# First attention step turned by TensorE, second step's keys gathered in layer 1, and two inverse roots taken as powers on GpSimd

## The chip, the cores and the metric

The kernel runs on one core of a Trainium2 chip. The core has five engines that run side by side and wait for one another only through semaphores: TensorE (PE, matrix products and transposes, which write to the PSUM memory), VectorE (DVE), ScalarE (ACT, among other things exponentials), GpSimd (POOL) and SyncE (SP, which here only issues DMA transfers). The profile keeps TensorE's loading of the stationary operand apart as PEld. The metric is the device time of one execution in microseconds (us), lower is better. The kernel before was timed three times.

## The reference, cut to what matters

The program is a chain of four layers over x, 8 sequences of 128 tokens with 512 features, all in float32. Layers 0 and 1 are feed-forward layers with low-rank experts, layer 2 is attention over a paged cache of keys and values followed by a small expert layer, layer 3 is again feed-forward. The change touches the end of layer 1 and the start of the attention:

```python
q = rmsnorm(x @ Wq.T) * q_norm_w          # 32 heads of 128
k = rmsnorm(x @ Wk.T) * k_norm_w          # 8 key heads of 128
v = x @ Wv.T
q, k = rope(q, pos), rope(k, pos)         # rotary: t * cos +- (other half of t) * sin
kc, vc = k_cache[block_table], v_cache[block_table]      # 512 cached positions
scores = q @ concat(kc, k).T / sqrt(128)
probs = softmax(where(valid, scores, -1e30))
x = x + layer(probs @ concat(vc, v) @ Wo.T)
# rmsnorm(t) = t * rsqrt(mean(t * t) + 1e-6)
```

## The kernel before

*Steps.* The attention runs in 32 steps, n = 0 to 31, each one key head (with its four query heads, REP) and a pair of sequences. A step needs, in this order: its projection (`project`, by a seven-product scheme written in `seven`, whose products are named q_one, q_six, q_five), the inverse root-mean-squares of its heads (`squares`, `roots`, `normed`), the rotation (`rotate`, `rotated`), the queries and new keys turned so that the head's 128 features lie along the partitions (`turn`, `fetch`), the cached keys gathered from the cache (`gather`, "kn") and turned likewise (`turn_cached`, "kt", "kT"), the score products (`weigh`, tile st, L1132) with their exponentials, and the mixing with the values (`mix`, tile av, L1184). The output products wo_one, wo_two and wo_six of step n - 1 stand between those of step n + 1's projection and the second half of step n.

*Order.* Nearly all attention instructions are issued with `keep_in_program_order`, so each engine runs them in the order of the text. The functions passed in the dictionary `at` (keys "one", "u2", "c22", "c11", "c12") are called by `seven` after the product of that name, and so say where on every engine's queue other work is put. `issue_after` keeps instructions behind a named one. Pools with `bufs` give a tile a new buffer only when its last users are done; the bank tags "av" (two), "st" and "mm" (three each) hold PSUM, and the tags "kt", "qT", "r" have one buffer each, "kn" two.

*Turning through memory.* VectorE's transpose works on blocks of 32x32. `turn` therefore transposes the blocks of `both` (eight query heads and two key heads, 128x1280) on VectorE, writes the result to a DRAM tensor in four DMAs (`written`, L1102), and `fetch` reads it back rearranged (L1119 for qT, L1122 for the keys kn). The cached keys go the same way (L1093, L1102, L1098).

*The transition (L1242 to L1299).* Layer 1's last steps interleave with the attention's start. `begin` loads weights and gathers step 0's keys and values on GpSimd. `first` projects step 0, turns its cached keys, gathers step 1's keys, starts to project step 1, and at "one" of that projection runs `rest`: squares and roots of step 0 on ScalarE, layer 1's last outputs (eo_l, added into x by VectorE at L300), rotation and norm of step 0, and its turning, for which half of the writes are issued by ScalarE. `run` then issues three matmuls into idle_q whose result is not used, the squares of step 1 on ScalarE, step 1's rotation, its cached keys, its roots, norm and turning, and then goes round the steps.

*Roots.* `roots` is a Sqrt on ScalarE (L1079), which needs another function table than Exp, and `normed` has VectorE's reciprocal (L1085) before the product with the queries (L1086). The key's root is the scale of the exponential of the new keys.

Of the kernel before, what the change touches and what calls it, by code (L numbers as in the profile page):

```python
# [10 lines left out]
F32 = mybir.dt.float32  # L11
I32 = mybir.dt.int32
AF = mybir.ActivationFunctionType
# [34 lines left out]
def forward(ctx: ExitStack, tc: tile.TileContext, a: dict, out: bass.AP):  # L48
# [252 lines left out]

    def block_masked(dst, ps, mask, g):

        dve.tensor_tensor(
            dst.rearrange("p (b t) -> p b t", t=P),
            ps.rearrange("p (b t) -> p b t", t=P),
            mask[:, 4 * g : 4 * g + 4].unsqueeze(2).to_broadcast([P, 4, P]),
            ALU.mult,
        )
# [358 lines left out]
    with psa:  # L668
        c2 = psa.enter_context(ExitStack())
        ps_ = psa.enter_context(tc.tile_pool(name="psa", bufs=2, space=PSUM, reuse_waits="tile"))  # L670
        sums = nc.dram_tensor("sums", (HQ * NB // REP, REP * P), F32, kind="Internal").ap()

        def small_bank(shape, name):
            return ps_.tile(shape, F32, tag="av", name=name)

        def large_bank(shape, name):
            return ps_.tile(shape, F32, tag="st", name=name, bufs=3)


        att = attention(tc, a, x, ident, lens, kvrow, part, ww, wop, ypool, sums, rot, eps, ps_, c2, chunks, mm)  # L680

        l1 = att.scratch([P, DC * P + NT], "l1")
        wa1 = l1[:, 0 : DC * P].rearrange("p (c r) -> p c r", c=DC)
        sp.dma_start(wa1, chunks(a["wa1"]))
        t1 = l1[:, DC * P : DC * P + NT]

        def adapt(g):
            tok = slice(g * 512, (g + 1) * 512)
            ps = small_bank([P, 512], f"t1_{g}")
            for c in range(DC):  # L690
                mm(ps, wa1[:, c, :], x[:, c, tok], c == 0, c == DC - 1)
            block_masked(t1[:, tok], ps, mask1, g)

        mids1, route1, mix1, outs1 = experts(
            "l1", None, None, 16.0, br.unsqueeze(1).to_broadcast([P, NB, 8]), wB1, None, None, add_to_x,
            mid_of=lambda tok: [(t1[:, tok], w11)],
        )[:4]

        mix0(0, large_bank)
        outs0(0, (0, 1), large_bank)  # L700
        mids0(1, small_bank)
        route0(1)
        outs0(0, (2, 3), large_bank)
        mix0(1, small_bank)
        outs0(1, (0, 1), large_bank)
        adapt(0)
        outs0(1, (2, 3), large_bank)
        mids1(0, small_bank)
        route1(0)
        att.begin()  # L710
        adapt(1)
        mix1(0, small_bank)
        outs1(0, range(DC), large_bank)
        mids1(1, small_bank)
        route1(1)
        att.first(lambda: mix1(1, small_bank), lambda *o: outs1(1, o, large_bank))
        kept = nc.dram_tensor("kept_x", (P, DC, NT), F32, kind="Internal").ap()
        c1.close()
        cl = ExitStack()
        late = cl.enter_context(tc.tile_pool(name="late", bufs=1, side="right"))  # L720

        def bank(tag, shape, name):
            return ps_.tile(shape, F32, tag=tag, name=name, bufs=2 if tag == "av" else 3)

        def room(tag, shape, name):

            return (ypool if tag == "y" else wop).tile(shape, F32, tag=tag, name=name)

        def end_of(in_order):
            return ending(  # L730
                tc, a, out, x, ident, bias3, experts, late,
                lambda shape, name: ww.tile(shape, F32, tag="q7", name=name),
                lambda shape, name: ww.tile(shape, F32, tag="qs", name=name), room, chunks, mm, in_order,
            )

        y2, end = att.run(late, end_of, bank, lambda: sp.dma_start(kept, x))
        c2.close()
        c3 = ExitStack()
        w3 = c3.enter_context(tc.tile_pool(name="w3", bufs=1, reuse_waits="tile"))
        ex["sm"] = c3.enter_context(tc.tile_pool(name="sm3", bufs=2, side="right", reuse_waits="tile"))  # L740
        end.open3(w3, ex["sm"])
        end.layer2(y2, bank, do=range(NB - 2, NB))
# [49 lines left out]
def attention(tc, a, x, ident, lens, kvrow, part, ww, wop, ypool, sums, rot, eps, psa, c2, chunks, mm):  # L792
# [39 lines left out]
        tabs[m] = (ws, wx)  # L832


    vals = []
    for k in range(4):
        vals.append(ap.tile([P, NC, HD], F32, tag=f"vals{k}", name=f"vals{k}"))
# [198 lines left out]
    def squares(n, m, j, heads):  # L1036

        for i in heads:
            sq = wk.tile([P, HD], F32, tag="sq", name=f"sq{m}_{n}_{j}_{i}", bufs=1)
            col = i if m == "q" else REP  # L1040
            kept(act.activation(sq, S[n][m][:, j, i, :], AF.Square, accum_out=S[n]["ssq"][:, j, col : col + 1]))  # L1041

    def rotate(n):

        both = wk.tile([P, 2 * REP + 2, HD], F32, tag="r", name=f"r_{n}", bufs=1)
        views = {"q": both[:, 0 : 2 * REP], "k": both[:, 2 * REP :]}

        def terms(m, t, nh):

            full = [P, 2, nh, HD]  # L1050
            ws, wx = (w[:, pair(n), :] for w in tabs[m])
            r = views[m].rearrange("p (j h) d -> p j h d", j=2)
            u = wk.tile(full, F32, tag="v" + m, name=f"v{m}_{n}", bufs=1)
            for b in ((slice(0, 1), slice(1, 2)) if nh > 1 else (slice(0, 2),)):
                for lo, hi in ((0, 64), (64, 0)):
                    to = u[:, b, :, lo : lo + 64]
                    kept(pool.tensor_tensor(  # L1057
                        to, t[:, b, :, hi : hi + 64],
                        wx[:, b, lo : lo + 64].unsqueeze(2).to_broadcast(list(to.shape)), ALU.mult,
                    ))  # L1060
            def straight_terms():
                kept(dve.tensor_tensor(r, t, ws.unsqueeze(2).to_broadcast(full), ALU.mult))

            S[n]["r" + m] = r, u
            return straight_terms

        S[n]["both"] = both
        terms("q", S[n]["q"], REP)()
        return terms("k", S[n]["k"], 1)
# [6 lines left out]
    def roots(n):  # L1076
        s = S[n]
        s["rs"] = rs = wk.tile([P, 2, REP + 1], F32, tag="rs", name=f"rs_{n}")
        kept(act.activation(rs, s["ssq"], AF.Sqrt, bias=eps, scale=1.0 / HD))  # L1079

    def normed(n):

        s = S[n]
        r, rs = s["rq"][0], s["rs"]
        kept(dve.reciprocal(rs, rs))  # L1085
        kept(dve.tensor_tensor(r, r, rs[:, :, 0:REP].unsqueeze(3).to_broadcast([P, 2, REP, HD]), ALU.mult))  # L1086

    def turn_cached(n, tag="kt"):

        s = S[n]  # L1090
        t = wk.tile([P, 4, 8, 32], F32, tag=tag, name=f"kt_{n}", bufs=1)
        for j in range(2):
            kept(dve.transpose(  # L1093
                t[:, :, 4 * j : 4 * j + 4, :], s["kc"][j].rearrange("p c (b d) -> p b c d", b=4)
            ))
        s["kT"] = wk.tile([P, 4, 8, 32], F32, tag="kT", name=f"kT_{n}")
        written(turned[n], t)
        return lambda: kept(sp.dma_start(s["kT"], turned[n].rearrange("b i a m d -> (b i) a m d")))  # L1098
# [13 lines left out]
        written(turned_new[n], t, by)  # L1112
        return done

    def fetch(n, between=lambda: None):
        s = S[n]
        m = 2 * REP
        src = turned_new[n].rearrange("b i a m d -> (b i) a m d")
        kept(sp.dma_start(s["qT"], src[:, :, 0:m, :]))  # L1119
        between()  # L1120
        for j in range(2):
            kept(sp.dma_start(s["kn"][:, j], src[:, :, m + j, :]))  # L1122

# [118 lines left out]
    def begin():  # L1242
# [3 lines left out]
        gather(0, "v")  # L1246
        every(W[0].factors())

    def first(mixed, outs_):

        every(tokens(0))
        running.append(True)
        later = tokens(1, "pT")
        project(0, {
            "u2": lambda: turn_cached(0)(),
            "c22": lambda: every(later),
            "c11": lambda: (squares(0, "k", 0, (0,)), squares(0, "q", 0, (0, 1))),
            "c12": lambda: squares(0, "q", 0, (2, 3)),
        })
        keys_terms = rotate(0)  # L1260
        gather(1, "k")
        mixed()

        def rest():
# [2 lines left out]
            roots(0)  # L1267
            keys_terms()
            outs_(0)
            rotated(0)  # L1270
            outs_(1)
            normed(0)
            turned_0 = turn(0, (sp, act))
            fetch(0)
            with tc.issue_after(turned_0.ins):
                outs_(2, 3)

        project(1, {"one": rest})

    def run(pool_, end_of, bank, keep):  # L1280
        late.append(pool_)
# [1 line left out]
        Y.append(y2)  # L1283
        pool.memset(y2, 0.0)

        idle = psa.tile([P, 512], F32, tag="mm", name="idle_q", bufs=3)
        for _ in range(3):
            kept(pe.matmul(idle, x[:, 0, 0:P], x[:, 0, 0:512], start=True, stop=True))
        for j in range(2):
            squares(1, "q", j, range(REP))  # L1290
            squares(1, "k", j, (0,))
        keys_terms = rotate(1)
        read_cached = turn_cached(1, "xs")
        keys_terms()
        gather(1, "v")
        roots(1)
        rotated(1)
        normed(1)
        turn(1)  # L1299
# [6 lines left out]
        for n, (qd, p) in enumerate(steps):  # L1306
# [40 lines left out]
            summed(n, 0)  # L1347
            if n == 0:
                next(sums_of)
                fetch(1, read_cached)  # L1350
                gather(2, "k")
            every(sums_of)
            summed(n, 1)
# [36 lines left out]
        leave(n)  # L1390
        return y2, end

    return SimpleNamespace(begin=begin, first=first, run=run, scratch=scratch)


def rotary(tc, rp, tp, lens, part, rows, kept):
# [898 lines left out]
```

## Time and profile before

| what | value |
|---|---|
| three runs | 1494.15, 1496.87, 1497.94 us; median 1496.87 |
| profiled execution | 1495.56 us, of which the span from first to last instruction is 1493.8 us |
| granted clock of TensorE | 0.999 of full speed |
| TensorE busy | 1479.5 us, 99% of the span |
| VectorE, GpSimd, ScalarE busy | 1069.0, 848.5 and 565.6 us |
| score products of step 0 and of step 1 begin | 324.01 and 341.25 us after the span's start |

TensorE is busy nearly always, so a microsecond elsewhere counts only where TensorE ends up waiting for it. A timeline line gives start, duration, engine, line, operation, output<-inputs, the shape and how many instructions were merged; in brackets stands how long the engine was idle before and what ended that idle time. The durations of TensorE's instructions are modelled ends: in a stream, the distance from one start to the next is what counts.

### The profile page before, as it was taken

What the parts mean: (1) busy time and instruction counts of PE and PEld (TensorE: products, weight loads), DVE (VectorE), ACT (ScalarE), POOL (GpSimd) and SP (SyncE); (2) the same over time, 40 slices, a digit from 0 to 9 for tenths busy, and PEclk for the clock granted to TensorE, in tenths of its full rate; (3) what the DMA queues carried; (4) which work ended last, traced back from release to release, by engine and by line L of the source; (5) the groups of instructions that cost most, each with busy time, mean ns of one, the idle gap of its engine ahead of it and who ended that gap; (6) DMA issues with size and microseconds to landing.
All of it is one profiled execution on the core that took longest, in us unless ns stands there. A gap on an engine that the chain in (4) does not pass through costs nothing.

```text
span 1493.8 us, 18138 instructions
## 1 busy us (share of the span) xinstructions
PE 1479.5 (99%) x5615; PEld 940.4 (63%) x5615; DVE 1069.0 (72%) x2121; ACT 565.6 (38%) x1432; POOL 848.5 (57%) x869
## 2 busy tenths in 40 slices
PE   9999999999999999999999999999999999999998
PEld 7888787445555655555555555565555565559887
DVE  4665425388888787787778778787868878854475
ACT  1111101054545554454554444554444455431110
POOL 2241104377776777776777777677777677621210
PEclk9999999999999999999999999999999999999999
DMA  7311001145546444564454455345445534432001
GB/s 242 117 43 32 1 1 56 50 119 143 176 139 189 148 116 128 154 184 125 134 152 131 129 155 179 109 135 163 129 131 159 166 107 138 120 113 87 2 5 55
DMA packets 159305, 174.05 MB, mean 117 GB/s; under 512 B 54752, under 2 KB 129696, under 8 KB 159072
## 3 DMA queue, kind: packets, MB, share of 16 engines
q1 hardware_dynamic: 140768, 135.47, 30.8%
q0 software_dynamic: 17056, 36.49, 7.6%
q10 hardware_dynamic: 1376, 0.85, 0.2%
q8 instruction: 47, 0.77, 0.2%
q14 instruction: 58, 0.48, 0.1%
HBM read 130.66 MB, written 42.07 MB: 116 GB/s over the span
## 4 chain that ended last, share of the span: by engine, by line
PE 94%; DVE 3%; issue 1%; DMA 1%; ACT 0%; POOL 0%; SPq 0%; DVEq 0%; ACTq 0%
PE st L1132 18%; PE av L1184 18%; PE q_six L968 8%; PE g L362 8%; PE wo_two L968 6%; PE q_one L968 5%; PE q_five L968 5%; PE dn L362 5%; PE wo_six L968 4%; PE wo_one L968 4%; PE eo_l L53 3%; PE h L1723 2%; PE z L1723 2%; PE o L1723 1%; PE midp_l L53 1%; PE gu L362 1%
## 5 line engine op out<-in xcount | busy, mean ns | idle before, releaser
L911 POOL DMA_INDIRECT kn<-in_k_cache,kvrow_k x256 | 272.7, 1065 | 73.3 <-issue 71.3
L911 POOL DMA_INDIRECT vals<-in_v_cache,kvrow_v x256 | 269.7, 1053 | 73.5 <-issue 61.3
L1184 PE MATMUL av<-pT,vals 128*128 128x512 f32 x640 | 290.6, 592 | 0.2 <-DVE oT L1194 0.2
L1136 ACT ACTIVATE pT<-st,hide 128x512 f32<-128x512 f32 x256 | 176.0, 687 | 194.2 <-PE st L1132 165.1
L1132 PE MATMUL st<-qT,kT 128*128 128x512 f32 x512 | 236.1, 594 | 1.7 <-DMA qT<-turned_new 1.6
L1184 PEld LDWEIGHTS av<-pT,vals 128*128 128x128 f32 x640 | 121.4, 190 | 153.1 <-issue 149.0
L1057 POOL TENSOR_TENSOR vq<-q,txq 128x256 f32<-128x256 f32 x128 | 119.8, 968 | 137.3 <-ACT sqq L1041 95.4
L1132 PEld LDWEIGHTS st<-qT,kT 128*128 128x128 f32 x512 | 96.4, 190 | 111.5 <-issue 106.9
L1152 DVE TENSOR_TENSOR part<-pT 128x512 f32<-128x512 f32 x128 | 88.2, 690 | 78.4 <-ACT pT L1136 60.5
L968 PE MATMUL q_one<-q,x 128*128 128x384 f32 x256 | 93.0, 486 | 0.0
L1041 ACT ACTIVATE sqq<-q 128x128 f32<-128x128 f32 x256 | 79.4, 310 | 11.0 <-DVE q L1017 3.7
L968 PEld LDWEIGHTS q_one<-q,x 128*128 128x128 f32 x256 | 48.5, 190 | 39.8 <-issue 14.1
L968 PE MATMUL q_six<-q_s,xs_all 128*128 128x384 f32 x192 | 69.8, 486 | 0.0
L1022 ACT COPY q<-q_one 128x256 f32<-128x256 f32 x32 | 11.9, 373 | 148.7 <-PE q_one L968 148.7
L968 PE MATMUL wo_one<-o,oT 128*128 128x256 f32 x256 | 65.8, 379 | 0.4 <-DVE oT L1194 0.4
L1132 PE MATMUL st<-qT,kTn 128*128 128x512 f32 x128 | 65.4, 592 | 0.0
L968 PE MATMUL wo_two<-o_s,os 128*128 128x256 f32 x256 | 60.5, 379 | 0.3 <-DVE os L927 0.3
L1136 ACT ACTIVATE pT<-st,rs 128x512 f32<-128x512 f32 x64 | 44.0, 687 | 38.4 <-PE av L1184 17.5
L968 PEld LDWEIGHTS wo_one<-o,oT 128*128 128x128 f32 x256 | 48.6, 190 | 14.0 <-DVE oT L1194 0.6
L429 POOL TENSOR_TENSOR ws<-wu 128x256 f32<-128x256 f32 (+1 forms) x9 | 6.5, 719 | 87.2 <-DMA wu<-in_WuT 80.6
L1168 ACT COPY rows<-rows 32x32 f32<-32x32 f32 x96 | 20.7, 216 | 93.1 <-DVE rows L1163 83.0
L362 PE MATMUL g<-xs,ws 128*128 128x256 f32 (+1 forms) x240 | 55.1, 379 | 0.0
(451 smaller groups left out, 2845.1 us busy)
## 6 DMA issues: line engine op xcount, KB each, us to landing
turned_new<-qkt SPq DMA_DIRECT2D x126, 160.0 KB
turned_cached<-kt SPq DMA_DIRECT2D x128, 128.0 KB
kT<-turned_cached SPq DMA_DIRECT2D x32, 512.0 KB
qT<-turned_new SPq DMA_DIRECT2D x32, 512.0 KB
R<-sums SPq DMA_DIRECT2D x32, 512.0 KB
q<-in_WqT SPq DMA_DIRECT2D x8, 1024.0 KB
o<-in_WoT SPq DMA_DIRECT2D x8, 1024.0 KB
kn<-in_k_cache,kvrow_k POOLq DMA_INDIRECT x256
```

The lines of the kernel that those rows point to most:

```text
L53: pe.matmul(o, lhsT, rhs, start=start, stop=stop)
L362: pe.matmul(o, lhsT, rhs, start=start, stop=stop, skip_group_check=True)
L911: kept(pool.indirect_dma_start(out=d[:, c, :], out_offset=None, in_=kc if what == "k" else vc, in_offset=bass.IndirectOffsetOnAxis(ap=kvro ...
L968: kept(pe.matmul(o, l[:, c, :], r[:, c, :], start=start and c == 0, stop=c == 1, skip_group_check=True))
L1041: kept(act.activation(sq, S[n][m][:, j, i, :], AF.Square, accum_out=S[n]["ssq"][:, j, col : col + 1]))
L1057: kept(pool.tensor_tensor(to, t[:, b, :, hi : hi + 64], wx[:, b, lo : lo + 64].unsqueeze(2).to_broadcast(list(to.shape)), ALU.mult,))
L1132: kept(pe.matmul(ps, s["kT"][:, c, 4 * j : 4 * j + 4, :] if c < 4 else s["kn"][:, j], s["qT"][:, :, REP * j : REP * (j + 1), :].rearrange( ...
L1136: kept(act.activation(pT[:, c, :, :].rearrange("p i t -> p (i t)"), ps, AF.Exp, **(dict(bias=hide[:, b, c : c + 1]) if c < 4 else dict(bia ...
L1152: kept(dve.tensor_tensor(o, l, r, ALU.add))
L1168: kept(act.copy(rows[0:32, g, :], rows[32 * g : 32 * g + 32, 0, :]))
L1184: kept(pe.matmul(ps, v[:, c, :], pT[:, c, :, :].rearrange("p i t -> p (i t)"), start=c == 0, stop=c == NC - 1, skip_group_check=True,))
L1723: return pe.matmul(o, lhsT, rhs, start=start, stop=stop, skip_group_check=True)
```

## The change

Four things are done.

- *Step 0's queries and keys are turned by TensorE.* `turn_at_once` transposes the ten 128x128 tiles of `both` with ten TensorE transposes into three PSUM tiles, and ScalarE copies them into qT and kn. It is called at "c11" of step 1's projection, which puts the transposes between the products q_one and q_five. Step 0's VectorE transposes and their DMAs are gone, and so are the three idle_q matmuls.
- *The cached keys come earlier.* Step 0's are transposed right behind layer 1's first masked product (`adapt(0)`), through the new function `begun`; step 1's are gathered there too, and are turned in the middle of step 0's projection, where step 0's were turned before.
- *The inverse roots of steps 0 and 1 are powers on GpSimd*: a multiply-add and a power of -0.5, on 128x10 each, behind the rotation terms in GpSimd's queue. Sqrt and reciprocal stay for the steps from 2 on.
- *The squares of step 1's second sequence and of its keys* are made by VectorE (`squared`: product and sum over the free axis) instead of ScalarE. ScalarE keeps those of the first sequence's four query heads.

In the changed order VectorE also adds layer 1's outputs eo 0 and eo 1 one behind the other, ahead of step 0's rotation sum.

```diff
-        adapt(0)
+        adapted = adapt(0)
         outs0(1, (2, 3), large_bank)
         mids1(0, small_bank)
         route1(0)
         att.begin()
+        att.begun(adapted)
...
+    half = ap.tile([P, 2, REP + 1], F32, tag="half", name="half")
+    pool.memset(half, -0.5)
...
+    def squared(n):
+        s = S[n]
+        sq = wk.tile([P, 2 * REP + 2, HD], F32, tag="kt", name=f"sq_{n}", bufs=1)
+        for v, here, to in (
+            (s["q"][:, 1], slice(0, REP), s["ssq"][:, 1, 0:REP]), (s["k"][:, :, 0], slice(REP, REP + 2), s["ssq"][:, :, REP])
+        ):
+            kept(dve.tensor_tensor(sq[:, here], v, v, ALU.mult))
+            kept(dve.tensor_reduce(to, sq[:, here], AX.X, ALU.add))
...
     def roots(n):
-        kept(act.activation(rs, s["ssq"], AF.Sqrt, bias=eps, scale=1.0 / HD))
+        if n < 2:
+            kept(pool.tensor_scalar(rs, s["ssq"], 1.0 / HD, EPS_RMS, ALU.mult, ALU.add))
+            kept(pool.tensor_tensor(rs, rs, half, ALU.pow))
+        else:
+            kept(act.activation(rs, s["ssq"], AF.Sqrt, bias=eps, scale=1.0 / HD))
...
-        kept(dve.reciprocal(rs, rs))
+        if n > 1:
+            kept(dve.reciprocal(rs, rs))
...
+    def turn_at_once(n):
+        s = S[n]
+        m = 2 * REP
+        s["qT"] = qT = wk.tile([P, 4, m, 32], F32, tag="qT", name=f"qT_{n}", bufs=1)
+        s["kn"] = kn = wk.tile([P, 2, 4, 32], F32, tag="kTn", name=f"kTn_{n}", bufs=1)
+        for h in (slice(0, REP), slice(REP, m), slice(m, m + 2)):
+            k = h.stop - h.start
+            ps = psa.tile([P, k, P], F32, name=f"turned_{n}_{h.start}", **(
+                dict(tag="av") if k == REP else dict(tag="st", bufs=3)
+            ))
+            for i in range(k):
+                kept(pe.transpose(ps[:, i, :], s["both"][:, h.start + i, :], ident))
+            to = qT[:, :, h, :].rearrange("p a m t -> p m a t") if k == REP else kn
+            kept(act.copy(to, ps.rearrange("p m (a t) -> p m a t", t=32)))
...
+    def begun(behind):
+        with tc.issue_after(behind.ins):
+            turn_cached(0)()
+        gather(1, "k")
...
         project(0, {
-            "u2": lambda: turn_cached(0)(),
+            "u2": lambda: turn_cached(1)(),
...
         keys_terms = rotate(0)
-        gather(1, "k")
         mixed()
...
             outs_(0)
+            outs_(1)
             rotated(0)
-            outs_(1)
             normed(0)
-            turned_0 = turn(0, (sp, act))
-            fetch(0)
-            with tc.issue_after(turned_0.ins):
-                outs_(2, 3)
-        project(1, {"one": rest})
+            outs_(2, 3)
+        project(1, {"one": rest, "c11": lambda: turn_at_once(0)})
...
-        idle = psa.tile([P, 512], F32, tag="mm", name="idle_q", bufs=3)
-        for _ in range(3):
-            kept(pe.matmul(idle, x[:, 0, 0:P], x[:, 0, 0:512], start=True, stop=True))
-        for j in range(2):
-            squares(1, "q", j, range(REP))
-            squares(1, "k", j, (0,))
+        squares(1, "q", 0, range(REP))
         keys_terms = rotate(1)
-        read_cached = turn_cached(1, "xs")
+        squared(1)
         keys_terms()
+        roots(1)
         gather(1, "v")
-        roots(1)
         rotated(1)
         normed(1)
         turn(1)
...
-                fetch(1, read_cached)
+                fetch(1)
```

## What I expected, before the changed kernel ran

> **What bounds the kernel.** I read the page first, then the waits of TensorE, then the chain of waits and the engines' timelines between 280 and 380 us, where the changed instructions lie.
>
> From the page, busy time by engine:
>
> ```profile
> PE 1479.5 (99%) x5615; PEld 940.4 (63%) x5615; DVE 1069.0 (72%) x2121; ACT 565.6 (38%) x1432; POOL 848.5 (57%) x869
> ```
>
> TensorE is the bound over the whole span, so only two things can pay: fewer matmuls, or the few microseconds in which TensorE waits. Its waits, longest first (total, times, longest):
>
> ```profile
> PE st L1132 <- DMA qT<-turned_new: 1.6, 1, 1.6
> ...
> PE q_six L968 <- DVE x L300: 1.1, 1, 1.1
> ```
>
> Both are in the stretch that the change rewrites. TensorE's timeline there (start, duration, and in brackets what it waited for):
>
> ```profile
> 307.11 3.60 PE L53 MATMUL eo_l<-midT_l,wB 128*128 128x512 f32 x8
> 311.77 1.56 PE L968 MATMUL q_six<-q_s,xs 128*128 128x384 f32 x4 [1.06 <-DVE x L300]
> ...
> 319.68 2.74 PE L1288 MATMUL idle_q<-x 128*128 128x512 f32 x6
> 324.01 3.67 PE L1132 MATMUL st<-qT,kT 128*128 128x512 f32 x8 [1.59 <-DMA qT<-turned_new]
> ...
> 341.25 3.60 PE L1132 MATMUL st<-qT,kT 128*128 128x512 f32 x8
> ```
>
> The reader is to see three losses: the wait for a PSUM bank that VectorE's addition into x must free, the dummy matmuls idle_q, and the wait for qT. After 324.01 no listed wait of TensorE in the steps is over 0.4 us; they follow each other every 32.2 us. The chain of waits into 324.01:
>
> ```profile
> 313.13 1.52 DVE qkt L1109
> 314.67 0.30 SPq L1102
> ...
> 319.34 4.53 DMA qT<-turned_new
> ```
>
> After VectorE has transposed its 32-blocks (qkt), two DMA trips follow: writing, from 314.67 until the read can be issued at 319.34, and reading, 4.53 until TensorE starts. Step 1 has the same trips (VectorE, then GpSimd, then the SP queue):
>
> ```profile
> 324.78 0.71 DVE L1093 STREAM_TRANSPOSE kt<-kn 128x512 f32<-128x512 f32 x1 [2.52 <-DMA kn<-in_k_cache,kvrow_k]
> ...
> 329.08 1.51 DVE L1109 STREAM_TRANSPOSE qkt<-r 128x1280 f32<-128x1280 f32 x1
> ...
> 320.48 1.98 POOL L911 DMA_INDIRECT kn<-in_k_cache,kvrow_k  x1 [0.30 <-issue]
> ...
> 334.95 0.53 SPq L1119 DMA_DIRECT2D qT<-turned_new  x1
> ```
>
> A gathered key tile is usable 2.3 us after the last gather's span on GpSimd ends (322.46 to 324.78). No TensorE wait is listed at 341.25, so step 1 is in time before the change.
>
> **What the Trainium skill says.** "VectorE: DVE Perf Modes", the three transpose paths: VectorE turns only 32x32 blocks, TensorE turns a whole 128x128 into PSUM. The trace agrees: qkt needs both DMA trips after it, midTp (four TensorE transposes) needs only a ScalarE copy. "DMA: Bandwidth & Descriptors", anatomy of one DMA: about 2.0 us fixed, most of it the receipt of the write. The trace has 4.3 to 4.7 us for each of the trips with their four issues or 512 KB. "TensorE: Matmul & The Clock Gate", Part 1: the clock falls only after an idle window of some 3.4 us, so idle_q can go if the new gaps stay short; here the granted clock stayed at 1.00 through the gap before 324.01. "GPSIMD Engine Reference", sections 2.1 and 3.1: about 2.6 cycles per element with two inputs, about 6 us at the first call of a freshly loaded kernel; it prices no power, and no run here shows one.
>
> **The change, part by part.**
>
> *Step 0 on TensorE.* In the changed order VectorE adds eo 0 and eo 1 one after the other at 308.2, so eo 1's bank is free near 309.7 instead of 311.7, and q_six can follow eo at 310.55 (307.11 + 8 x 0.43) instead of 311.77. Then q_six, q_five, q_six and q_one, 4 x 1.29, end at 315.71. Ten transposes come in: midTp's four take 0.44 in the chain, 0.108 each, so 1.08, to 316.79. Two more products, to 319.37, and st follows: idle_q is gone. qT must be there: ScalarE copies q and k out (0.37 + 0.27) from 315.9, then turned (two of 128x512 at 0.59 as midT, one of 128x256 near 0.4), done near 318.0. kT was turned in layer 1 and landed long before; Exp's table is still loaded, since Sqrt is gone, so ScalarE's two table loads of 1.28 go too. They were hidden. So st starts at 319.37 instead of 324.01: **4.64 gained**.
>
> *Its cover.* The r x rs product waits for GpSimd: vk ends at 310.65, then a multiply-add on 10 elements (0.25, estimated from memsets of 0.1 plus dispatch) and the power, p. Queued behind it on VectorE are eo 2 (0.69), eo 3 (0.6) and two uq sums (1.1), the last of which frees q_five at 316.79. So r x rs (1.24) must start by about 313.0; with p = 1 it starts at 312.2. Up to p = 1.9 step 0 pays nothing, above that one for one.
>
> *p* is bounded below by a small instruction on GpSimd (0.1) and above by the skill's first-call price (6) if the code must be loaded, or some 13 if the 160 values of each core are evaluated one by one at an assumed 100 cycles. I take 1.0: ten vectors of a core's 16 partitions, some hundred cycles each. These are estimates with the page's 16 lanes of a core and 1.2 GHz.
>
> *Step 1's queries.* They still take the DMA trips. VectorE: q's last sum at 319.57 instead of 319.88; r x tsq from 320.1, 1.6 rather than 1.22 since GpSimd now multiplies beside it (as in step 2, 1.61); then four new operations: squares 128x512 (0.69), their sum (0.69), squares 128x256 (0.43), their sum (0.4), to 323.9 with their gaps; the key term 0.55, then 1.3 and 0.4, to 326.05. The two kt transposes and their wait of 2.52 are gone from here, moved to layer 1's stretch (kt 0 at 278.8, where VectorE idles over 3 us; kt 1 at 300.9 in kt 0's place). GpSimd: vq from 318.75 (its 10 us of key gathers now lie at 280 to 290, ahead of the memset of y, 3.5, which is needed only near 358), vk to 323.4, power to 324.2 + p: hidden up to p = 1.8. Then 1.24 + 1.51: qkt ends at 328.85, against 330.6. The SP queue writes four times and issues qT 4.5 later, 333.35; landed 4.53 later, 337.9. TensorE wants it at 319.37 + 17.24 = 336.61. On SP, kt 0's four writes now pass the load of o, at 280, and kT 0's read follows it at 285.8; both have 30 us to spare. **Stall 1.4**, bounds 0.5 (trip of 4.3 and 3.9) and 2.2 (the product of 1.6 or a trip grows). kT no longer shares this burst: 512 KB less, the reason I don't go higher. The gap of 1.4 is under the window in which the clock falls.
>
> *Step 2's keys.* GpSimd's value gathers for step 1 start at 325.35 instead of 326.40, and the key gathers behind them take as long as before (12.27 + 11.23), so they end at 348.85, usable near 351.15. VectorE wants them for its second kt transpose at 352.73 - 3.24 = 349.5. It stands 1.65 in that transpose, and behind it are o_s, q and vals from q_five, which free the bank of wo_two: 352.9, against 352.2 wanted. **Stall 0.75**, bounds 0 and 1.2. After this POOL again waits for VectorE, and the steps run at 32.2 as before; qT of step 2 has 5.18 from issue to use and needs about 4.5.
>
> The squares and table loads removed from ScalarE, VectorE's qkt of step 0 (1.51), the SP writes and reads of step 0 and the two reciprocals (0.2) were off TensorE's path after these waits; nothing is added for them.
>
> Sum: 4.64 - 1.4 - 0.75 = **2.5 us**. The profiled execution took 1495.56 (span 1493.8 and 1.8 around it); it would take 1493.1. It lies 1.3 below the median of the three runs, 1496.87; from the median I get **1494.4**.
>
> **Rivals.** *(a) Step 1 and 2 are in time*: trips as short as step 1's 4.33 and quick gathers give the whole 4.6, 1492.3. For it: the DMA engines carry 512 KB less. Against: qT's chain gains 1.7 us where TensorE gains 4.6. *(b) The power is slow, slower than before.* Step 0 then loses p - 1.9, and step 2's keys come later by p - 1 more, so the gain is 2.5 - (p - 1) - (p - 1.9) = 5.4 - 2p. It turns at p = 2.7; p = 5 gives 1501.5, p = 13 gives 1517. If only the first call costs 6: 2.5 - 4.1, 1498.5. For it: no GpSimd row here is anything but an add, a multiply or a memset, and VectorE stands behind it with the bank releases. Against: 10 elements per partition only. *(c) The stalls are larger but p is small*: SP's four writes meet the value gathers, a trip of 5.2 each, gain near 1 us, 1495.9.
>
> **How the numbers follow.** Forecast (gain 1.5 to 3.5) 0.50; (a) 0.16; (c) and nothing 0.14; (b) with p between 2.7 and 5 or a first call only, 0.08; (b) beyond, 0.12. About 0.3% (4.5 us) can be told from no change. (a) reaches it only with luck of the runs, whose three values spread by 3.8: faster 0.10. Slower beyond 0.3% is (b) beyond, and a share of unknown: 0.15. Same 0.75. The range, 1490.8 to 1500.0, takes (a) with 1.5 of run spread below, and above reaches into (b) up to p near 4.2.
>
> **What would show it.** Right: st of step 0 near 319.4 with no wait and no idle_q; qT of step 1 named as TensorE's wait, about 1.4 at 336.6; a VectorE wait for kn near 349; power rows on GpSimd near 1 us. Wrong: a power above 2 us and turned waiting for r; a wait of st 0 for ScalarE's copies; a gap at 310.6; step 2 without a VectorE wait for kn.

## The result and the profile after

| | before | after |
|---|---|---|
| median | 1499.16 us (16 runs) | 1503.26 us (16 runs) |
| profiled execution, span | 1493.8 us | 1503.5 us |
| granted clock in the profiled execution | 0.999 | 0.995 |
| end of layer 0's last product eo_l<-y,base (285.18 / 289.58) to st of step 0 | 38.83 us | 38.74 us |
| st of step 0 to st of step 1 | 17.24 us | 20.50 us |
| st of step 1 to st of step 2 | 32.24 us | 34.04 us |

The ratio is 1.0033, with a 95% interval of 1.0018 to 1.0049: the change costs 4.9 us (2.7 to 7.3) where 2.5 us of gain was predicted. (The means of the runs differ by 5.0 us, the medians by 4.1.) The two profiled spans differ by more, 9.7 us. Of that, 4.4 us lie ahead of 285.18 in work of TensorE that the change doesn't touch, and vary from run to run: in the profiles of the experiments below the same point lies between 285.6 and 289.7, and both of these ends come from kernels built on the one before. From st of step 2 to the end of the span the two executions take nearly the same, 1120.3 and 1120.6 us. The three distances in the table lie between these two points. They sum to 88.31 and 93.28 us, a loss of 5.0, which is the measured loss, and they are what the rest of this text compares.

TensorE's busy line in the page of the kernel after, against 1479.5 us before:

```profile
PE 1482.2 (99%) x5619; PEld 943.2 (63%) x5619; DVE 1072.2 (71%) x2122; ACT 561.0 (37%) x1419; POOL 853.2 (57%) x874
```

Its list of TensorE's waits (total, times, longest):

```profile
PE st L1165 <- DMA qT<-turned_new: 4.0, 2, 3.2
PE midTp_l L283 <- DVE mw_l L272: 3.3, 1, 3.3
```

Both waits of before are gone: x for q_six, and qT in step 0. A wait of 3.3 us has come that was not in the forecast at all, and qT's wait has moved to step 1 and is 3.2 us (the other 0.8 us of its line are at 1159.8, far behind this stretch). The timeline of TensorE after:

```profile
298.56 1.09 PE L283 MATMUL midTp_l<-ident,mw_l 128*128 128x128 f32 x4 [3.26 <-DVE mw_l L272]
...
300.38 4.40 PE L53 MATMUL eo_l<-midT_l,wB 128*128 128x512 f32 x8
...
319.49 1.45 PE L971 MATMUL q_six<-q_s,xs 128*128 128x384 f32 x4
...
324.65 1.25 PE L1145 MATMUL turned<-ident,r 128*128 128x128 f32 x10
...
328.32 3.60 PE L1165 MATMUL st<-qT,kT 128*128 128x512 f32 x8
...
348.82 5.40 PE L1165 MATMUL st<-qT,kT 128*128 128x512 f32 x8 [3.17 <-DMA qT<-turned_new]
```

Step 0 is as predicted: q_six follows eo_l without a wait, the ten transposes cost 1.09 us, and st starts without a wait. But eo_l took 4.40 us behind the first wait (3.60 before), and st of step 1 5.40 us instead of 3.60. The table of stretches of the kernel after shows a lower clock there (start:end, length, then each engine's busy time; PEclk, the granted clock, is the third figure from the end):

```profile
298.50:305.08 6.58, 6.52 (x20) 4.15 (x21) 3.15 (x6) 0.97 (x2) 0.00 (x0) 0.75 0.00 0
305.08:348.80 43.72, 40.57 (x120) 20.93 (x118) 35.62 (x66) 17.43 (x53) 25.82 (x25) 1.00 0.23 65
348.80:354.90 6.10, 6.08 (x10) 2.58 (x11) 4.53 (x10) 2.70 (x4) 4.75 (x5) 0.72 0.41 141
```

Behind each of the two waits TensorE works some 6 us at a mean clock of 0.75 and 0.72. So each wait is paid twice: 3.26 and then about 1.45 (from midTp_l at 298.56 to q_one at 305.08 is 6.52 us, the same work before took 5.41 with a wait of 0.34 in it, so 1.45 more); 3.17 and then 1.8 (st to q_one is 6.09 us, before 4.29).

**Where the first wait comes from.** The timeline of all engines after, ahead of midTp_l:

```profile
292.75 0.94 POOL L914 DMA_INDIRECT kn<-in_k_cache,kvrow_k  x1 [0.30 <-issue]
292.92 0.19 DVE L267 TENSOR_REDUCE s_l<-e_l 128x4 f32<-128x32 f32 x1 [0.29 <-ACT e_l L250]
293.14 4.11 DVE L268 TENSOR_SCALAR s_l<-s_l 128x4 f32<-128x4 f32 x1
293.69 3.54 POOL L1319 MEMSET y<- 128x4096 f32 x1
297.28 0.18 DVE L269 RECIPROCAL s_l<-s_l 128x4 f32<-128x4 f32 x1
```

The tensor_scalar on four elements per partition, part of layer 1's expert weights, takes 4.11 us and ends at 297.25, 0.02 us behind the memset of y. Now the eight moved key gathers stand ahead of that memset on GpSimd, and it runs from 293.69 to 297.23. Behind the tensor_scalar on VectorE comes mw_l, the experts' values times their weights, and TensorE's midTp_l, which transposes mw_l, waits for it. The memset, the tensor_scalar and TensorE's work behind them in the kernel before:

```profile
285.45 3.52 POOL L1284 MEMSET y<- 128x4096 f32 x1 [9.82 <-issue]
288.73 0.26 DVE L268 TENSOR_SCALAR s_l<-s_l 128x4 f32<-128x4 f32 x1
...
290.73 0.60 PE L283 MATMUL midTp_l<-ident,mw_l 128*128 128x128 f32 x4
...
292.24 3.60 PE L53 MATMUL eo_l<-midT_l,wB 128*128 128x512 f32 x8
```

There too the tensor_scalar ended 0.02 us behind the memset (288.99 and 288.97), but it came when the memset was nearly done, so that this cost it 0.09 us only (it takes 0.17 with no memset beside it). The text ahead of the prediction says that the engines wait for one another only through semaphores. The experiments below show an exception: the two instructions have no tile in common, and the profile lists no wait of VectorE here, only an instruction that takes 4.11 us.

**Where the second comes from.** The chain of waits after, through step 1's queries (start, duration, what):

```profile
333.64 2.82 POOL rs L1094
...
336.49 1.24 DVE r L1104
...
337.75 1.52 DVE qkt L1127
...
340.60 3.26 DMA turned_new<-qkt
...
344.00 4.69 DMA qT<-turned_new
```

The power takes 2.81 us, VectorE waits 1.51 us for it ahead of the product with r, and the two DMA trips, to DRAM and back, follow.

### The profile page after: what moved, and what is told of

The parts are those of the page before. It is cut to its first block, busy times and chain, and to the rows that moved or that the text cites. A ratio compares the mean times of both kernels' runs of the same rounds, so it can differ in the third digit from the quotient of the medians.

```text
span 1503.5 us, 18126 instructions
## 1 busy us (share of the span) xinstructions
PE 1482.2 (99%) x5619; PEld 943.2 (63%) x5619; DVE 1072.2 (71%) x2122; ACT 561.0 (37%) x1419; POOL 853.2 (57%) x874
## 4 chain that ended last, share of the span: by engine, by line
PE 91%; DVE 4%; DMA 3%; issue 1%; ACT 0%; POOL 0%; SPq 0%; ACTq 0%; DVEq 0%; POOLq 0%
PE st L1165 17%; PE av L1217 17%; PE g L362 8%; PE q_six L971 8%; PE q_one L971 5%; PE q_five L971 5%; PE wo_two L971 5%; PE dn L362 5%; PE wo_six L971 4%; PE wo_one L971 4%; PE eo_l L53 3%; PE h L1753 2%; PE z L1753 2%; PE o L1753 1%; PE midp_l L53 1%; DMA adapter_ids_i<-in_adapter_ids 1%
## 5 line engine op out<-in xcount | busy, mean ns | idle before, releaser
L1201 ACT COPY rows<-rows 32x32 f32<-32x32 f32 x96 | 20.7, 216 | 97.4 <-DVE rows L1196 78.4
```

The lines of the kernel that those rows point to most:

```text
L1201: kept(act.copy(rows[0:32, g, :], rows[32 * g : 32 * g + 32, 0, :]))
```

## The experiments

Theory M says that the pushed-back memset made the first wait; its rival G lays it to the gathers themselves. Theory Q says that step 1's DMA trips, behind a power that is late (P), made the second; rivals are V (the rotated queries are late anyway) and D (the trips alone count). Theory C says that the waits themselves lower the clock, H that something else does.

**1. The memset elsewhere** (k1). Everything else is the changed kernel.

```diff
             roots(0)
+            y2 = ypool.tile([P, NB, D], F32, tag="y", name="y2")
+            Y.append(y2)
+            kept(pool.memset(y2, 0.0))
             keys_terms()
...
-        y2 = ypool.tile([P, NB, D], F32, tag="y", name="y2")
-        Y.append(y2)
-        pool.memset(y2, 0.0)
+        y2 = Y[0]
```

> The changed kernel, with the memset of y moved behind step 0's power in GpSimd's queue (where GpSimd waits 5.8 us for step 1's q). Theory M (the memset, pushed behind the eight moved key gathers, holds VectorE's tensor_scalar on s_l, and TensorE waits behind it): the tensor_scalar on s_l takes 0.2 to 0.3 us instead of 4.11, TensorE waits under 0.5 us for the first midTp_l instead of 3.26, and from the last eo_l<-y,base to st of step 0 it is 34.1 us instead of 38.74; the time falls by 4.7 us against the changed kernel. Rival G (the gathers' own work on GpSimd holds VectorE): the gathers stand where they stood, so the tensor_scalar still takes about 4 us and the distance stays at 38.7. The wait of 3.2 us for step 1's qT stays under both.

Measured: ratio to the kernel before 1.0003 (0.9995 to 1.0011), so 4.5 us better than the changed kernel's 1.0033. The timeline:

```profile
289.49 0.17 DVE L268 TENSOR_SCALAR s_l<-s_l 128x4 f32<-128x4 f32 x1
...
291.49 0.60 PE L283 MATMUL midTp_l<-ident,mw_l 128*128 128x128 f32 x4
```

There is no wait for midTp_l, and from the end of eo_l<-y,base (285.94) to st of step 0 (320.15) it is 34.21 us, 4.5 less than after and 4.62 less than before. The gathers ran as they had, one of them (288.73 to 289.67) beside the tensor_scalar, so it was not they. The wait for step 1's qT stayed at 3.19 us, and st of step 2 comes 34.32 us behind that of step 1.

**2. The memset made longer in the kernel before** (k2).

```diff
         pool.memset(y2, 0.0)
+        pool.memset(y2, 0.0)
```

> The kernel before, its memset of y issued twice in a row, so that GpSimd fills memory from 285.4 to about 292.5, over the tensor_scalar on s_l (288.73). Theory M: the tensor_scalar takes about 3.8 us (until the second memset ends) instead of 0.26, the first midTp_l starts 1.3 us after the memset's end, so TensorE waits about 3 us there, the granted clock falls behind it for some 5 us (another 1 to 1.5 us), and st of step 0 comes 4 us later; the time rises by 4 us. Rival G (only gathers do this): the tensor_scalar stays under 0.5 us and nothing moves.

Measured: ratio 1.0003 (0.9994 to 1.0013), nothing moved, against M as it was put. The timeline shows why the run can't decide:

```profile
285.91 3.52 POOL L1284 MEMSET y<- 128x4096 f32 x1 [9.84 <-issue]
...
289.19 0.26 DVE L268 TENSOR_SCALAR s_l<-s_l 128x4 f32<-128x4 f32 x1
289.48 3.52 POOL L1285 MEMSET y<- 128x4096 f32 x1
```

The tensor_scalar came 0.24 us before the end of the first memset, and ended at 289.45, 0.02 behind that end and ahead of the second one's start. If it is held, then only by an instruction in progress; here it slipped in between the two.

**3. A memset that is in progress** (k8), the sharper form of the same.

```diff
+        pool.memset(y2[:, 0 : NB // 2], 0.0)
         pool.memset(y2, 0.0)
```

> The kernel before with a memset of half of y put ahead of the whole one, so that a GpSimd memset is in progress when VectorE comes to the tensor_scalar on s_l (289.2): the half fills 285.9 to 287.7, the whole 287.7 to 291.2. Theory M: the tensor_scalar ends with the whole memset, at 291.2 to 291.3, so takes 2.0 us instead of 0.26; midTp_l starts 1.3 us behind that and TensorE waits 1.4 us; since the gap is short the granted clock stays at 1.00, and the time rises by 1 us only. Rival G (only gathers hold VectorE, or the memset does only together with one): 0.2 to 0.3 us.

Measured: ratio 1.0015 (1.0004 to 1.0026).

```profile
291.79 3.52 POOL L1285 MEMSET y<- 128x4096 f32 x1
...
293.21 2.12 DVE L268 TENSOR_SCALAR s_l<-s_l 128x4 f32<-128x4 f32 x1
...
296.64 0.63 PE L283 MATMUL midTp_l<-ident,mw_l 128*128 128x128 f32 x4 [1.28 <-DVE mw_l L272]
```

The row of the stretch behind that wait:

```profile
296.60:302.00 5.40, 5.24 (x21) 3.04 (x22) 3.13 (x6) 0.97 (x2) 0.00 (x0) 1.00 0.00 0
```

In the kernel before, with no gather near, the tensor_scalar took 2.12 us and ended at 295.33, 0.02 behind the memset's end at 295.31. TensorE waited 1.28 us, the clock stayed at 1.00 in the 5.4 us behind it, and st of step 0 came 40.26 us behind the end of eo_l<-y,base, 1.43 more than before. M is shown in both directions: taken out of the changed kernel, put into the one before.

**4. Step 1 turned by TensorE too** (k3), in the changed kernel, with the memset where it was. The three PSUM tiles of the turning all have the tag st in step 1.

```diff
-        turn(1)
...
-                fetch(1)
                 gather(2, "k")
...
                 every(tokens(2))
+                turn_at_once(1)
```

> The changed kernel with step 1's queries and keys turned by TensorE too (ten transposes ahead of the mixing of step 0's second sequence, no DRAM trip). Theory Q (step 1's st waits for the two DMA trips behind a late power): the wait for qT is gone, st of step 1 comes 17.24 + 1.1 = 18.3 us after st of step 0 instead of 20.50, and st of step 1 to the first q_one behind it is back at 4.3 us instead of 6.09; together 4.0 us less. Rival V (the power or the vq products are what is late, so that the rotated queries themselves come too late): TensorE waits for r or for the copies of qT by 1 to 3 us, and the distance stays at 19.5 or more. Rival H (the low clock after 348.8 is not caused by the gap): the distance falls but st to q_one stays near 6 us.

Measured: ratio 1.0032 (1.0022 to 1.0042), hardly a gain. The timeline of this kernel:

```profile
345.24 3.70 PE L1165 MATMUL st<-qT,kT 128*128 128x512 f32 x8 [0.71 <-ACT qT L1147]
...
358.45 0.71 DVE L1111 STREAM_TRANSPOSE kt<-kn 128x512 f32<-128x512 f32 x1 [1.53 <-DMA kn<-in_k_cache,kvrow_k]
...
360.41 0.89 PE L971 MATMUL wo_two<-o_s,os 128*128 128x256 f32 x3 [0.72 <-DVE vals L1020]
```

The DMA wait is gone and the clock is whole again (st to q_one 4.40 us), so H falls for this stretch. The 0.71 us that TensorE still waits, for the copies, stay under the 1 to 3 us of V, so Q stands. But st of step 1 is 19.13 us behind st of step 0, not 18.3, because the copies to qT stood behind ScalarE's row copies (L1201), which wait for VectorE until 344.0. And st of step 2 comes 34.45 us later: VectorE waits 1.53 us for step 2's keys, TensorE 0.72 us for the sums that stand behind that on VectorE, and 0.99 us for step 2's qT (st at 379.69). From step 0's to step 2's st it is 53.58 us against 54.54 after. The late keys had been hidden by the late step 1.

**5. Dummy products in the wait** (k4), otherwise the changed kernel.

```diff
+            if n == 0:
+                idle = psa.tile([P, 512], F32, tag="mm", name="idle_st", bufs=3)
+                for _ in range(3):
+                    kept(pe.matmul(idle, x[:, 0, 0:P], x[:, 0, 0:512], start=True, stop=True))
             next(prepared, None)
             if n and p == 0:
```

> The changed kernel with three matmuls of 128x512 whose result is not used put ahead of step 1's st, into the wait for qT. Theory C (the idle gap of 3.2 us is what lowers the granted clock): the gap shrinks to about 0.6 us, st of step 1 starts where it did (20.5 us after st of step 0), and from it to the first q_one takes 4.3 us instead of 6.09, so 1.8 us less in all. Rival H (the clock falls for another reason, or falls after any wait): 6 us stay and the time is unchanged.

Measured: ratio 1.0022 (1.0012 to 1.0031), against 1.0033. The two intervals overlap, so the gain is read from the profile, and the runs only agree with it.

```profile
343.36 2.74 PE L1401 MATMUL idle_st<-x 128*128 128x512 f32 x6
346.61 3.70 PE L1165 MATMUL st<-qT,kT 128*128 128x512 f32 x8 [0.52 <-DMA qT<-turned_new]
...
351.01 1.45 PE L971 MATMUL q_one<-q,x 128*128 128x384 f32 x4
```

The row of the stretch from st to q_one:

```profile
346.60:351.00 4.40, 4.39 (x10) 2.01 (x11) 4.26 (x11) 2.72 (x4) 3.49 (x4) 1.00 0.31 83
```

st of step 1 starts 20.42 us behind that of step 0, as late as without them, but takes its full speed: 4.40 us to q_one instead of 6.09. C holds: 1.7 us of the second wait's price is the clock, and products whose result is not used save it. Whether idle_q did the same in the kernel before, where it stands right ahead of the wait of 1.59 us for qT, is likely but not shown: no run took it out there alone.

**6. Step 1's power twice** (k7), on top of k1.

```diff
+            if n == 1:
+                again = wk.tile([P, 2, REP + 1], F32, tag="again", name="again")
+                kept(pool.tensor_tensor(again, rs, half, ALU.pow))
             kept(pool.tensor_tensor(rs, rs, half, ALU.pow))
```

> k1 (the changed kernel with the memset of y moved) with step 1's power taken twice, the first time into a tile that nothing reads. Theory P (the power sets when step 1's queries leave): VectorE's product of r and rs waits 1.5 + 2.8 = 4.3 us for GpSimd, TensorE's wait for qT grows from 3.19 to 6.0 us, st of step 1 comes 23.3 us behind st of step 0. Rival D (the two DMA trips or other traffic set it, and the power has slack): the wait for qT grows by less than 1.5 us.

Measured: ratio 1.0030 (1.0023 to 1.0038). The timeline:

```profile
325.65 2.81 POOL L1096 TENSOR_TENSOR again<-rs,half 128x10 f32<-128x10 f32 x1
...
328.54 1.96 POOL L1097 TENSOR_TENSOR rs<-rs,half 128x10 f32<-128x10 f32 x1
...
330.53 1.23 DVE L1107 TENSOR_TENSOR r<-r,rs 128x1024 f32<-128x1024 f32 x1 [3.55 <-POOL rs L1097]
...
342.75 5.77 PE L1168 MATMUL st<-qT,kT 128*128 128x512 f32 x8 [5.09 <-DMA qT<-turned_new]
```

The second power took 1.96 us, VectorE's wait grew by 2.04 (from 1.52 in k1 to 3.55) and TensorE's wait for qT by 1.90 (from 3.19 to 5.09). What is added to the power arrives at TensorE nearly whole: P stands, and D, which allowed less than 1.5, falls. The rise was put at 2.8, since the first power's duration was taken for the second; that one runs while VectorE waits, the first beside VectorE's sums into r.

**7. All three mended** (k5): the memset as in k1; step 1 turned by TensorE, its copies ahead of the row copies; and step 1's value gathers in GpSimd's idle stretch, so that step 2's keys are early.

```diff
         gather(1, "k")
+        gather(1, "v")
...
         roots(1)
-        gather(1, "v")
...
-        turn(1)
...
-                fetch(1)
+                turn_at_once(1)
                 gather(2, "k")
```

> The changed kernel with three edits: the memset of y behind step 0's power; step 1's value gathers moved up behind its key gathers, into GpSimd's idle stretch in layer 1, so that step 2's key gathers come some 10 us earlier; and step 1's queries and keys turned by TensorE, their ScalarE copies ahead of the row copies. All the mechanisms named so far must hold at once: the tensor_scalar on s_l of both routings takes 0.2 us (the value gathers then run over the second one; if gathers hold VectorE it takes 0.4 us or more), no TensorE wait over 0.5 us from there to step 3, st of step 1 is 18.3 us behind st of step 0 and st of step 2 32.2 us behind that. From k1's ratio of 1.0003 and its 54.8 us from st of step 0 to st of step 2, now 50.5: ratio 0.9975, 3.8 us faster than before. Rival: another transfer or engine takes the place of the waits removed (VectorE, which still does step 1's squares), and the ratio stays at 0.999 to 1.001.

Measured: 1494.70 us, ratio 0.9981 (0.9971 to 0.9991), 2.8 us under the kernel before and some 7.8 under the changed one; the expected ratio was 0.9975. The timeline:

```profile
299.53 0.94 POOL L914 DMA_INDIRECT vals<-in_v_cache,kvrow_v  x1 [0.30 <-issue]
...
299.95 0.17 DVE L268 TENSOR_SCALAR s_l<-s_l 128x4 f32<-128x4 f32 x1
...
320.77 3.60 PE L1165 MATMUL st<-qT,kT 128*128 128x512 f32 x8
...
339.03 3.60 PE L1165 MATMUL st<-qT,kT 128*128 128x512 f32 x8
...
371.80 3.70 PE L1165 MATMUL st<-qT,kT 128*128 128x512 f32 x8 [0.25 <-DMA qT<-turned_new]
```

A tensor_scalar in the middle of a gather takes 0.17 us, so a gather alone doesn't hold it. st of step 1 is 18.26 us behind st of step 0 without a wait, st of step 2 another 32.77 behind that, 0.5 more than before, half of it a wait for qT. No wait of TensorE in this stretch is over 0.35 us. Step 1's power takes as long here (2.82 us) and VectorE waits for it as before (1.52), so this delay reaches TensorE only together with the DMA trips behind it.

The three distances of all kernels, in us, beside the runs (ratio less 1, times some 1498 us):

| kernel | eo_l to st 0 | st 0 to st 1 | st 1 to st 2 | sum less before | by the runs |
|---|---|---|---|---|---|
| before | 38.83 | 17.24 | 32.24 | 0 | 0 |
| after | 38.74 | 20.50 | 34.04 | +5.0 | +4.9 |
| k1 memset later | 34.21 | 20.52 | 34.32 | +0.7 | +0.4 |
| k2 before, memset twice | 39.11 | 17.24 | 32.24 | +0.3 | +0.4 |
| k8 before, half first | 40.26 | 17.24 | 32.24 | +1.4 | +2.2 |
| k3 step 1 on TensorE | 38.45 | 19.13 | 34.45 | +3.7 | +4.8 |
| k4 dummy products | 38.49 | 20.42 | 32.35 | +3.0 | +3.3 |
| k7 power twice | 34.21 | 22.42 | 34.41 | +2.7 | +4.5 |
| k5 all three | 34.21 | 18.26 | 32.77 | -3.1 | -2.8 |

All but k7's lie within the interval of the runs; k7's sum lies 0.7 below its interval's lower end. Its profile is that of the fastest of its 19 runs (1498.85 us, the median is 1501.60), and in it the part behind st of step 2 takes no longer than before (1119.9 us); where the rest lies stays open.

## Why the prediction was wrong

**Step 0 on TensorE: right.** Predicted 4.64 us; k1, in which nothing else disturbs the stretch, gained 4.62. The ten transposes cost 1.09 against 1.08.

**The failed step: the moved key gathers.** The prediction had them "now lie at 280 to 290, ahead of the memset of y, 3.5, which is needed only near 358", and costed the move at nothing. It asked who needs the memset's result, not what runs beside it at its new place. The place itself was right: the gathers ran from 284.0 to 293.7 in a profile whose layer 0 ended 4.4 us later. The memset behind them fell on the tensor_scalar of layer 1's routing, which then waited for its end. Cost by k1: 38.74 less 34.21, 4.5 us, of which some 3.3 is the wait and the rest the clock. That took back all of step 0's gain. The Trainium skill states the mechanism, in "SBUF — State Buffer", "Who interferes with whom": a tensor_scalar can take the port pair that VectorE shares with GpSimd, and the one that has it holds it for its whole instruction, the other waits. The trace agrees: in the profiles of after, k3, k4 and k8 the held tensor_scalar ends 0.02 to 0.03 us behind the memset. That it is this port pair no run here shows. One thing differs: the section lets the first to issue have the pair, and after the change the tensor_scalar's recorded start is 0.55 us ahead of the memset's, with a gather in between; which of them held it in that time stays open.

**Step 1's stall: right in kind, too small.** Predicted 1.4 us with bounds of 0.5 and 2.2; st of step 1 came 3.26 later than before (20.50 less 17.24), of which 3.17 is a listed wait. The prediction's own times (qT landed at 337.9, wanted at 336.61) give 1.3. Two terms were mis-sized. The power, taken as 1.0 and "hidden up to p = 1.8", took 2.81, and it began 5.3 us behind st of step 0 instead of 4.8 (VectorE's squares, on which it works, ended 0.3 us later than put); so VectorE waited 1.51. The trips, 4.5 and 4.53, took 4.71 and 4.82. That is 1.3 + 1.5 + 0.5, what was seen. k7 shows that the power's time goes through to TensorE.

**The clock: wrong, through the stall.** "The gap of 1.4 is under the window in which the clock falls" fits k8, where a gap of 1.28 left the clock whole. The gaps that came, 3.26 and 3.17, did not leave it so, and cost 1.45 and 1.8. The prediction let idle_q go on the condition that "the new gaps stay short", and put nothing for the case that they don't; in k4 such products got 1.7 back.

**Step 2's keys: the mechanism was right, but hidden.** No stall came after the change, as TensorE was late itself. In k3, where it was less late, the wait of wo_two behind kt appeared with 0.72 us against the 0.75 predicted, VectorE's with 1.53 against 1.65. A wait for step 2's qT, which the prediction had excluded, came in k3 too, with 0.99.

**Cover in step 0: right in the result, with luck.** The limit had been put at a power of 1.9; it took 2.04, and the multiply-add ahead of it 1.00 instead of the 0.25 assumed (0.23 in step 1; why is not shown). What made up for it is that GpSimd's two products for the key (vk) took 0.87 us, where the prediction had taken over 1.84 from the kernel before, so that GpSimd was free 1.0 us sooner. VectorE waited 1.90 us for the power; its product of r and rs began 5.98 us behind the start of eo_l, where the prediction's times give 5.9 as the last moment (313.0 less 307.11), and TensorE did not notice.

In sum: 4.6 gained, 4.5 lost to the memset, 3.3 to step 1's qT (20.50 less 17.24) and 1.8 to the clock behind it: 5.0 lost. Forecast and result lie 7.5 us apart: 4.5 from the memset, 1.9 from the larger stall, 1.8 from the clock, less the 0.75 put for step 2's keys, which did not come. Of the rivals, (b) named the power as the danger, but let it cost through step 0 and step 2's keys, with the turn at 2.7 us; it cost through step 1's queries. The largest part came from an instruction that no rival named.

## What to carry to other kernels

When work is moved ahead of something on a queue, price what it pushes back by what runs beside it at its new place, not only by when its result is due; on GpSimd, look for tensor_scalar instructions of VectorE under every long memset. Here TensorE's waits near 3 us were paid again in the clock behind them, so shorten or fill such a wait, with products whose result is not used if need be, before taking such fillers out. A late engine hides the next late transfer: after one wait is mended, look for the one behind it before counting the gain.

## What the hardware showed that was not expected

- A VectorE tensor_scalar of 128x4 (0.17 us) took 4.11, 3.72, 3.74 and 2.12 us (after, k3, k4, k8), each time to the end of a GpSimd memset; a reduction (0.18 us at 287.81 in the kernel before) and products with two inputs such as r by rs (1.23 us beside the moved memset in k5) were not held. A gather on GpSimd alone did not hold it (0.17 us in k1 and k5).
- TensorE's clock fell to a mean of 0.72 to 0.75 over the next 6 us behind listed waits of 2.88 (k3), 2.90 (k4), 3.17 and 3.26 us (after) and 3.19 us (k1), and stayed at 1.00 behind 1.28 (k8) and 1.88 (k2). "TensorE: Matmul & The Clock Gate", Part 1, gives a free-running window of some 3.4 us (one that no wait starts); here shorter listed waits were enough. The waits are measured from modelled ends of the products before them; counted from the spacing of their starts, 0.43 us each, the shortest is 3.1 us.
- A GpSimd power on 128x10 took 1.96 to 2.05 us where VectorE added beside it for less than 0.2 us, and 2.81 or 2.82 where it did for 1.3 us, in every profile; that the additions are the cause is not shown. The first power of the program, 2.04 or 2.05 us, was not the dearest.
